# Two graph layers on one core: the second layer's sum over edges as a two by two block product in seven multiplications

## The chip, the core and the metric

The kernel runs on one core of a Trainium2 chip. A core has TensorE (PE; its weight loads are listed apart as PEld), VectorE (DVE), ScalarE (ACT), GpSimd (POOL) and the queue engine SyncE (SP), which here issues nearly all DMAs. The metric is the device time of one execution in microseconds (us), as a median over runs. "Clock" is the share of TensorE's full clock that the chip granted.

## The reference, cut to what matters

There are 1250 nodes with 1024 features and 20000 edges with a weight each.

```python
h = relu(layernorm(x))
x = x + L0(h)      # sigmoid(h @ wenc.T + benc) -> @ conv, weighted sum over edges, + h @ lin.T -> @ wdec.T + bdec
h = relu(layernorm(x))
x = x + L1(h)      # h @ W.T + b, then over edges and self loops: sum of deg^-1/2[row] * deg^-1/2[col] * (row of col)
```

With C the 1250 x 1250 matrix that counts the edges between two nodes (plus the identity, for the self loops), D the diagonal of deg^-1/2 and y = D h, the second layer is D (C y) W.T, plus a term for the bias. The product C y, 1250 x 1250 by 1250 x 1024, is the second layer's sum over edges. It is taken before the product with W.

## The kernel before, in words

All of the work is on tiles of 125 nodes (T = 125, NT = 10 of them). Operands of float32 products are split into a high and a low part (a copy into float32r and a subtraction), and a product takes three passes: high by high, high by low, low by high. Counts are small integers and have no low part, so C y takes two passes.

1. *Encoder, to about 83 us.* Rows are loaded, normed, transposed on TensorE and multiplied by wenc, in five chunks of two tiles. The order of work is written out by hand (`ORDER`).
2. *lin, conv, and the first layer's sum over edges ("agg"), to about 246 us.* Between these products the matrices of weights and of counts are built (`edge_work`: `one_hots` on VectorE, L453 to L461; `adjacency` on TensorE, L479 to L484, then copies on ScalarE and VectorE, L494 to L504). Each 125 columns of counts are stored to HBM (`c_d<-cnt`).
3. *Decoder, to about 308 us.* For each tile t two products with wdec of 512 columns; VectorE adds them to x (L819), takes the statistics (L233), and ScalarE writes relu of the normed row (L249, tile `yf`), copies it as y's high part (L838), and VectorE takes the low part (L799). The sum x is stored to HBM as `x1_d` for the end.
4. *Second layer.* For each of five chunks c of 250 nodes `gathered(c)` multiplies y (stationary, eight blocks of 128 features, ten tiles, two parts) by the chunk's transposed counts `ct` (moving, 250 columns): 160 matmuls on L874. The result z is split (L885, L886), and `finish(c)` multiplies it by w1 (L926, 512 columns), adds and stores (L945). The counts of the next chunk are loaded, transposed on TensorE (L770) and copied (L773) between these products; `bias_factor` (L780) takes a row's sum of counts times the degrees' factor.

Outside of the encoder a planner orders the instructions of each engine by its costs, ahead of the run; on the chip each engine then takes its own list in order. SBUF is given out by two sets of equal slots, 18 big (`big`, 8000 to 8192 bytes a partition) and 14 middle ones (`mid`), in the order of the program: a slot is taken again as soon as its last user has given it back.

```python
def tile(self, shape, dtype, name):
    i = self.free.pop(0)
    t = mem.tile(shape, dtype, tag=f"{self.tag}{i}", name=name)
```

PSUM has eight banks: four for products (`ps_acc`), two for transposes (`ps_t`), two for the edges' matrices (`ps_oh`).

Of the kernel before, what the change touches and what calls it, by code (L numbers as in the profile page):

```python
"""Two pre-norm graph layers on one core.  # L1

Layer 0 (weighted graph convolution inside an encoder and decoder) and layer 1 (a symmetrically
normalised one with self loops) both sum over the same edges, as products with the edges' dense
matrices of weights and of counts.

The matrices are built in SBUF. Destinations go in groups of five, and each group takes a window of
128 consecutive edges, which starts at the first edge that is not below the group when the edges are
sorted by destination. A window's product of one-hot rows, of a source's place among 125 on one side
and of (destination, source's block of 125) times the weight on the other, is the group's columns.  # L10
The weight goes in three bf16 parts that add up to it exactly. The edges that the windows hold are
counted: where they are not all of the edges (unsorted or very uneven destinations), a second path,
for edges in any order, computes the output.

Operands of float32 products are split exactly into a high and a low part of 12 significant bits
each, which TensorE takes in one pass as float32r; counts need no low part.
"""
# [9 lines left out]
F32 = mybir.dt.float32  # L27
# [11 lines left out]
N_BIG = 18  # L39
N_MID = 14  # L40
WARM = 18

# What goes between the encoder's products, after (-1: before) part n of chunk c's: (c, n).
# [30 lines left out]
}  # L74


@with_exitstack
def kernel(
# [36 lines left out]

    const = ctx.enter_context(tc.tile_pool(name="const", bufs=1))
    mem = ctx.enter_context(tc.tile_pool(name="mem", bufs=1))
# [6 lines left out]
    class Slots:  # L124
        """Equal pieces of SBUF, handed out and given back in the order of the program."""

        def __init__(self, tag, n):
            self.tag = tag
            self.free = list(range(n))
            self.of = {}  # L130

        def tile(self, shape, dtype, name):
            i = self.free.pop(0)
            t = mem.tile(shape, dtype, tag=f"{self.tag}{i}", name=name)
            self.of[name] = i
            return t
# [1236 lines left out]
```

## Time and profile before

| | |
|---|---|
| three runs | 523.43, 523.54 and 525.04 us; median 523.54 us |
| profiled execution | 525.9 us from the first to the last instruction; no other time of it is listed |
| PE, PEld busy | 502.7, 456.5 us |
| DVE, ACT, POOL busy | 290.7, 166.1, 73.5 us |
| mean granted TensorE clock | 0.978 |
| C y (L874) | 800 matmuls of 250 columns |
| product with w1 (L926) | 456 matmuls of 512 columns, 48 of 256 |
| DMA | 48.89 MB, mean 93 GB/s |

Matmuls overlap, so the mean duration of one (282 ns for 250 columns) is longer than the time from one to the next; that time is read from the chain of waits, which lists stretches of matmuls with their count and length. The chain follows the work that ended last backwards. A wait names what ended an engine's idle time. In the view by stage each column is the busy time of an engine in that stretch.

### The profile page before, as it was taken

To read this page: it belongs to the slowest core of one execution; us is meant where nothing else is said; L and a number is where in the kernel's file an instruction comes from. 1 tells how busy PE (TensorE), PEld (TensorE's weight loads), DVE (VectorE), ACT (ScalarE), POOL (GpSimd) and SP (SyncE) were. 2 spreads that over 40 slices of the span, in tenths; PEclk is the share of its full clock that TensorE was granted. 3 is DMA by queue.
4 is the path that set the end of the run, shared out by engine and by line. 5 is a ranking of instruction groups with operands and counts; after the bars stand their busy time and mean duration, and the time that the engine had idled before them with its cause. 6 is when DMAs were issued, how large, how long until landed. Compare 5 with 4: busy or idle time off the path is not lost.

```text
span 525.9 us, 9741 instructions
## 1 busy us (share of the span) xinstructions
PE 502.7 (96%) x3954; PEld 456.5 (87%) x3954; DVE 290.7 (55%) x706; ACT 166.1 (32%) x432; POOL 73.5 (14%) x97
## 2 busy tenths in 40 slices
PE   6999997999999996899999998999999999999994
PEld 3999997998889996899777798889889879979984
DVE  6768579657788886662677675544044016115201
ACT  4676453543434343230155543301111111110100
POOL 5723560000000004130012340000000000000000
PEclk9999998999999999699999998999999999999999
DMA  8990120111011122744438452341024015004002
GB/s 294 355 261 22 31 77 0 27 26 26 1 26 26 51 81 64 166 123 106 153 127 255 177 185 67 118 141 68 0 77 131 1 40 167 1 21 115 24 12 73
DMA packets 37781, 48.89 MB, mean 93 GB/s; under 512 B 16608, under 2 KB 26472, under 8 KB 37727
## 3 DMA queue, kind: packets, MB, share of 16 engines
q1 hardware_dynamic: 37407, 47.79, 30.2%
q8 instruction: 33, 0.54, 0.4%
q0 software_dynamic: 320, 0.39, 0.3%
q14 instruction: 21, 0.17, 0.1%
HBM read 34.61 MB, written 17.37 MB: 99 GB/s over the span
## 4 chain that ended last, share of the span: by engine, by line
PE 82%; DVE 7%; DMA 6%; ACT 1%; issue 1%; SPq 0%; POOL 0%; ACTq 0%; DVEq 0%; POOLq 0%
PE pout L926 21%; PE pz L874 16%; PE pagg L318 10%; PE pdec L318 10%; PE penc L318 6%; PE plin L318 5%; PE pconv L318 4%; DMA c_d<-cnt 3%; PE penc L549 2%; PE poh L479 2%; PE pt L258 2%; DVE oh L457 1%; DVE oh L453 1%; PE pct L770 1%; PE poh L483 1%; PE poh L484 1%
## 5 line engine op out<-in xcount | busy, mean ns | idle before, releaser
L926 PE MATMUL pout<-w,z 128*125 128x512 f32 (+1 forms) x504 | 117.6, 388 | 0.0
L926 PEld LDWEIGHTS pout<-w,z 128*125 128x125 f32 x504 | 87.9, 186 | 18.9
L874 PE MATMUL pz<-ct,y 125*128 125x250 f32 x800 | 96.2, 282 | 2.0 <-ACT y L838 2.0
L874 PEld LDWEIGHTS pz<-ct,y 125*128 125x128 f32 x800 | 95.6, 191 | 2.7 <-ACT y L838 2.2
L318 PE MATMUL pagg<-A,h 125*125 125x250 f32 x600 | 76.5, 287 | 0.0
L318 PEld LDWEIGHTS pagg<-A,h 125*125 125x125 f32 x600 | 73.7, 193 | 0.0
L318 PE MATMUL pdec<-wdec,agg 126*125 126x512 f32 x240 | 57.7, 398 | 0.0
L945 DVE SCALAR_TENSOR_TENSOR res<-pout,dinv,res 125x512 f32<-125x512 f32 (+1 forms) x21 | 15.2, 724 | 71.7 <-PE pout L926 71.7
L318 PEld LDWEIGHTS pdec<-wdec,agg 126*125 126x125 f32 x240 | 44.3, 187 | 10.8
L885 ACT CAST z<-pz 128x250 fp32r<-128x250 f32 x40 | 14.3, 370 | 93.0 <-PE pz L874 73.8
L453 DVE TENSOR_TENSOR oh<-cols,eb 128x640 bf16<-128x640 bf16 x50 | 27.0, 539 | 28.1 <-DMA c_d<-cnt 20.6
L479 PE MATMUL poh<-oh 128*128 128x100 bf16 x250 | 28.9, 208 | 10.0 <-DVE A L504 7.3
L494 ACT CAST A<-poh 125x100 fp32r<-125x100 f32 x150 | 25.5, 258 | 40.3 <-PE poh L484 40.1
L318 PE MATMUL penc<-hnh,wenc 128*125 128x250 f32 x256 | 35.4, 288 | 0.0
L886 DVE TENSOR_TENSOR z<-pz,z 128x250 fp32r<-128x250 f32 x40 | 15.9, 413 | 34.7 <-ACT z L885 34.7
L479 PEld LDWEIGHTS <-oh 128*128 128x128 bf16 x250 | 24.1, 97 | 11.6 <-issue 8.0
L773 ACT CAST ct<-pct 125x500 fp32r<-125x500 bf16 (+1 forms) x30 | 15.1, 507 | 55.2 <-PE pct L770 52.4
L318 PEld LDWEIGHTS penc<-hnh,wenc 128*125 128x125 f32 x256 | 32.2, 191 | 0.0
L318 PE MATMUL plin<-hT,lin 125*125 125x250 f32 x240 | 31.0, 285 | 0.0
L318 PEld LDWEIGHTS plin<-hT,lin 125*125 125x125 f32 x240 | 29.4, 191 | 0.0
L318 PE MATMUL pconv<-conv,hT 125*125 125x500 f32 x120 | 28.5, 391 | 0.0
L483 PE MATMUL poh<-oh 128*128 128x50 bf16 x250 | 28.0, 190 | 0.0
(148 smaller groups left out, 689.0 us busy)
## 6 DMA issues: line engine op xcount, KB each, us to landing
x<-in_x_dram SPq DMA_DIRECT2D x14, 512.0 KB
x_d<-x SPq DMA_DIRECT2D x9, 512.0 KB
res<-x_d SPq DMA_DIRECT2D x9, 512.0 KB
out_dram<-res SPq DMA_DIRECT2D x19, 224.0 KB
c_d<-cnt SPq DMA_DIRECT2D x10, 312.5 KB
cr<-c_d SPq DMA_DIRECT2D x10, 312.5 KB
x<-in_x_dram SPq DMA_DIRECT2D x8, 256.0 KB
wencf<-in_wencT_dram SPq DMA_DIRECT2D x4, 500.0 KB
```

What stands on the lines that cost most here:

```text
L258: nc.tensor.transpose(p[:, k, :], xs[t][:T, kk * P : (kk + 1) * P], ident[:T, :T])
L318: nc.tensor.matmul(p, left[i], right[j], start=(part == 0 and n == 0), stop=(part == 2 and n == len(terms) - 1),)
L453: nc.vector.tensor_tensor(pairs(bo), pairs(cols).unsqueeze(1).to_broadcast([P, PB, P // 2, 2]), eb[:, gs].unsqueeze(2).to_broadcast([P, PB ...
L479: nc.tensor.matmul(p[:, g, :], left, mv[:, g, 0:2, :].rearrange("p q m -> p (q m)"), start=True, stop=False,)
L483: nc.tensor.matmul(p[:, g, M:], left, mv[:, g, 2, :], start=False, stop=False)
L494: nc.scalar.copy(hi, whole)
L773: nc.scalar.copy(ct[c][q][:, :, i * T : (i + 1) * T], p[:T, :m, :T])
L874: nc.tensor.matmul(ps[m][:, :CH], y[k][:, s, m * P : (m + 1) * P], ct[c][k // 4][:, k % 4, :], start=(k == 0 and s == 0), stop=(k == NT - ...
L885: nc.scalar.copy(zt[:, 0, m % 2, :], p[:, :CH])
L886: nc.vector.tensor_sub(zt[:, 1, m % 2, :], p[:, :CH], zt[:, 0, m % 2, :])
L926: nc.tensor.matmul(ps[u][:T, : cs.stop - cs.start], z[c][m // 2][:, i, m % 2, (t % 2) * T : (t % 2 + 1) * T], w1[m][:, j, cs], start=(m == ...
L945: nc.vector.scalar_tensor_tensor(x1[t][:, cs], ps[u][:T, : cs.stop - cs.start], dinv[:, t : t + 1], x1[t][:, cs], op0=OP.mult, op1=OP.add,)
```

## The change

C and y are each divided into two by two blocks: C by odd and even tiles of destination and source, y's tiles by odd and even and its features by halves. The product of the blocks is computed by Strassen's scheme in Winograd's form, seven block products in place of eight, with sums of blocks on either side. A block product has five tiles in the sum (NP = 5), 626 columns of counts (625 and one of zeros, W) in pieces of 312 and 314, and is made for four blocks of 128 features (KH = 4).

- *Counts.* The three blocks 11, 21, 22 and the four sums s1 to s4 are made during the decoder, all of them before the products begin: transposes on TensorE, copies on ScalarE, differences s1 and s3 on VectorE, s2 and s4 on GpSimd. `bias_factor` of all tiles moves from the second layer into the decoder.
- *y.* The decoder writes relu straight into one large tile `yz` in float32. The high and low parts are made later, for each of the 28 block products (`prepare`, five products ahead), with the sums of y's blocks on GpSimd first; for the first five the part of tiles 0 to 7 goes ahead of the rest.
- *Products.* `product_step` accumulates the seven products of a feature block in six banks: x and y in `ps_acc`, z in `ps_oh`, with held copies u1 to u3 in SBUF, and writes z in float32, for all 1250 nodes, in the place of y. Only then comes the product with w1, with z split by tile (`split_rows`). w1 is loaded and split during the last seven block products instead of in the decoder and after it.
- *SBUF.* The slots give way to one arena with a list of 322 offsets (`PLAN`), one for each tile in the order of the program, for all stages of the kernel. The code of the encoder, of the edges' matrices and of the first layer is otherwise the same.
- The path for edges in any order, which is in a branch that these inputs don't take, gets some reads and a barrier at its start.

```diff
+class Arena:
+    def tile(self, shape, dtype, name):
+        at = 32 * next(self.places, 0)
...
+        t = self.nc.alloc_sbuf_tensor_at(
+            f"{name}_{len(self.nc.cur_bb.bb.instructions)}", list(shape), dtype, offset=self.base + at
+        )
...
+    NP = NT // 2
+    W = NP * T + 1
...
+    def counts(block, h):
+        q, i = int(block[0]) - 1, int(block[1]) - 1
+        rows_ = cr[2 * h + i]
+        p = ps_t.tile([P, NP, T + 1], BF16, tag="pt", name="pct")
+        for k in range(NP):
+            nc.tensor.transpose(
+                p[:T, k, :T], rows_[:T, (2 * k + q) * T : (2 * k + q + 1) * T], ident_b[:T, :T]
+            )
...
+        if block != "12":
+            nc.scalar.copy(ct[block][:, :, hs], v)
+            return
+        nc.vector.tensor_sub(ct["s1"][:, :, hs], v, ct["11"][:, :, hs])
+        nc.vector.tensor_sub(ct["s3"][:, :, hs], ct["22"][:, :, hs], v)
...
+    def count_sums(s, h):
+        hs = slice(h * T, (h + 1) * T)
+        a, b = {"s2": ("22", "s1"), "s4": ("21", "s2")}[s]
+        nc.gpsimd.tensor_sub(ct[s][:, :, hs], ct[a][:, :, hs], ct[b][:, :, hs])
...
+    for h in range(NP):
+        order += [("11", h), ("21", h), ("22", h)]
+    for h, when in enumerate((9, 13, 16, 18, 19)):
+        order.insert(when, ("12", h))
+    for n, (block, h) in enumerate(order):
+        steps[n].append(lambda block=block, h=h: counts(block, h))
+        if block == "21":
+            steps[n].append(lambda h=h: (bias_factor(2 * h), arena.give(f"cr{2 * h}")))
+        if block == "22":
+            steps[n].append(lambda h=h: bias_factor(2 * h + 1))
...
-            if 5 <= t < 8:
-                counts(0, 2 * (t - 5) + half)
+            for step in steps[2 * t + half]:
+                step()
...
-        yf[t] = mid.tile([T, D], F32, f"yf{t}")
-        y[t] = big.tile([T, 2, D], FR, f"y{t}")
-        relu(yf[t], xt, rs)
-        nc.scalar.copy(y[t][:, 0], yf[t])
+        relu(y[:, :, t], xt.rearrange("p (h m f) -> p m h f", h=2, m=KH), rs)
...
+    count_sums("s2", NP - 1)
+    begin_counts("s4")
+    for h in range(NP):
+        count_sums("s4", h)
+    BLOCKS = {1: ("11", "11"), 2: ("12", "21"), 3: ("s4", "22"), 4: ("22", "s4"), 5: ("s1", "s1"),
+              6: ("s2", "s2"), 7: ("s3", "s3")}
+    Y_SUMS = {"s1": ("21", "22", OP.add), "s2": ("s1", "11", OP.subtract),
+              "s4": ("12", "s2", OP.subtract), "s3": ("11", "21", OP.subtract)}
+    def prepare(m, n, pieces=((0, NP),)):
...
+        for j0, j1 in pieces:
+            for s in {"s2": ("s1", "s2"), "s4": ("s4",), "s3": ("s3",)}.get(name, ()):
+                a, b, op = Y_SUMS[s]
+                nc.gpsimd.tensor_tensor(
+                    sums[m, s][:, j0:j1], y_block(m, a)[:, j0:j1], y_block(m, b)[:, j0:j1], op=op
+                )
+            v, to = y_block(m, name)[:, j0:j1], left[m, n]
+            nc.scalar.copy(to[:, 0, j0:j1], v)
+            nc.vector.tensor_sub(to[:, 1, j0:j1], v, to[:, 0, j0:j1])
...
+    PIECES = ((0, W // 2 - 1), (W // 2 - 1, W))
+    def multiply(m, which, key, first, last):
+        right = ct[BLOCKS[which][1]]
+        for n, (c0, c1) in enumerate(PIECES):
+            p = bank(m, n, key)
+            for j in range(NP):
+                for s in range(2):
+                    nc.tensor.matmul(
+                        p, left[m, which][:, s, j, :], right[:, j, c0:c1],
...
+    def product_step(m, which):
+        if which == 1:
+            multiply(m, 1, "x", True, False)
+            hold(m, "u1", "x")
+        elif which == 2:
+            multiply(m, 2, "x", False, True)
+            put(m, 0, 0, "x")
+        elif which == 6:
+            multiply(m, 6, "y", True, False)
+            hold(m, "u2", "y", "u1")
+        elif which == 5:
+            multiply(m, 5, "z", True, False)
+        elif which == 7:
+            multiply(m, 7, "y", False, False)
+            hold(m, "u3", "y", "u1")
+            put(m, 1, 1, "z", "u3")
...
+        elif which == 3:
+            multiply(m, 3, "z", False, True)
+            put(m, 0, 1, "z", "u2")
...
+        elif which == 4:
+            multiply(m, 4, "y", False, True)
+            put(m, 1, 0, "y", "u1")
...
+    products = [(0, 1), (1, 1), (0, 2)]
+    for m in range(KH):
+        products += [(m, 6), (m, 5), (m, 7)]
+        if 0 < m < KH - 1:
+            products.append((m + 1, 1))
+        products += [(m, 3), (m, 4)]
+        if m + 1 < KH:
+            products.append((m + 1, 2))
+    AHEAD = 5
...
+        if i >= len(products) - 7:
+            for _ in range(2):
+                if len(splits) > len(loads):
+                    k = splits.pop(0)
+                    split_w1(k, nc.gpsimd if k < KH else nc.vector)
+            for _ in range(2 if i < len(products) - 1 else 0):
+                if loads:
+                    load_w1(loads.pop(0))
...
+    def split_rows(t, m0, m1):
+        i, h = t % 2, t // 2
...
+            v, to = z[m][:, :, ns], zs[t][:, :, :, m]
+            nc.scalar.copy(to[:, 0], v)
+            nc.vector.tensor_sub(to[:, 1], v, to[:, 0])
```

## The prediction

> **What bounds the kernel now.** I read the page first, then the chain of waits by line, the waits of TensorE alone, and the busy time by stage.
>
> ```profile
> span 525.9 us, 9741 instructions
> PE 502.7 (96%) x3954; PEld 456.5 (87%) x3954; DVE 290.7 (55%) x706; ACT 166.1 (32%) x432; POOL 73.5 (14%) x97
> ...
> PEclk9999998999999999699999998999999999999999
> ```
>
> TensorE is busy almost throughout, but "busy" counts overlapping matmuls, so the pace is taken from the chain, which walks through one chunk of the second layer:
>
> ```profile
> 344.55 5.62 PE pout L926 x24
> 350.17 18.73 PE pz L874 x160
> ```
>
> 160 matmuls of 250 columns in 18.73 us are 117 ns each; 24 of 512 columns in 5.62 us are 234 ns each. TensorE waits for others in few places (us, times, longest):
>
> ```profile
> PE poh L479 <- DVE A L504: 7.3, 4, 4.7
> PE pt L258 <- ACT x L249: 3.1, 2, 2.2
> PE poh L479 <- DVE oh L461: 2.7, 1, 2.7
> PE pz L874 <- ACT y L838: 2.0, 1, 2.0
> ```
>
> By stage (window; its length; PE, PEld, DVE, ACT, POOL busy; granted clock; DMA):
>
> ```profile
> 77.00:87.00 10.00, 7.33 (x61) 7.12 (x61) 10.00 (x23) 2.17 (x8) 2.95 (x2) 0.83 0.00 0
> 203.00:221.00 18.00, 11.35 (x97) 11.03 (x96) 11.81 (x22) 5.65 (x16) 7.26 (x3) 0.72 0.50 133
> 246.00:314.00 68.00, 68.00 (x351) 56.24 (x350) 48.14 (x92) 28.07 (x30) 17.01 (x14) 1.00 0.52 173
> 314.00:327.00 13.00, 10.99 (x84) 10.78 (x83) 5.06 (x10) 5.31 (x10) 0.12 (x1) 0.87 0.14 34
> 327.00:519.50 192.50, 191.98 (x1216) 169.09 (x1214) 60.41 (x126) 26.18 (x59) 0.00 (x0) 1.00 0.22 69
> ```
>
> So there are three holes, and each brings a spell at half clock. **Hole A** (80 us): 2.7 us idle and 3.4 us at half clock, which costs 1.7: 4.4 us. **Hole B** (205 us): 4.7 + 1.95 idle, and 7 busy us at half clock, 3.5: 10 us. **Hole C** (315 us): 2.0 + 1.7 = 3.7 us. Everything else follows the number of columns. The timelines of VectorE and GpSimd show what hole B is:
>
> ```profile
> 204.94 2.36 POOL L602 TENSOR_TENSOR wdec<-wdec0f,wdec 126x1024 fp32r<-126x1024 f32 x1 [17.15 <-issue]
> ...
> 205.65 2.00 DVE L453 TENSOR_TENSOR oh<-cols,eb 128x640 bf16<-128x640 bf16 x1 [4.27 <-DMA c_d<-cnt]
> 207.57 2.43 DVE L457 TENSOR_TENSOR oh<-cols,ed 128x250 bf16<-128x250 bf16 x1
> ...
> 210.38 2.10 DVE L674 TENSOR_TENSOR agg<-hl,agg 125x250 fp32r<-125x250 f32 x1
> ```
>
> A one-hot first waits 4.27 us for a slot of SBUF that a store of counts still reads; then the same operations that take 0.49, 0.28 and 0.42 us elsewhere take 2.0 to 2.4 us, until a GpSimd split ends. Hole A is the same: the splits of conv and lin hold VectorE between 70 and 80 us.
>
> **What the Trainium skill says.** "SBUF — State Buffer", Who interferes with whom: a VectorE instruction with two SBUF inputs and a GpSimd one that reads SBUF exclude each other, one with an input from PSUM does not. The trace agrees: L674 took 2.10 instead of 0.42 us, L819 (from PSUM) 0.69 us under a split as without. "TensorE: Matmul & The Clock Gate", HAM oscillation: idle gaps over some 3.4 us halve the clock; here 2.0 us did. The same page, LDWEIGHTS: 128 columns load in 128/1.2 = 107 ns, so a 250-column matmul just covers its load and a wider one has room; in the trace the loads of L874 are busy 95.6 of its 96.2 us, those of L926 87.9 of 117.6. "GPSIMD Engine Reference", Instruction dispatch: about 2.5 cycles an element for two inputs; the trace has 2.40 us for 1024, 2.34 ns each, which I use.
>
> **The change part by part.**
>
> *Products.* 800 matmuls of 250 columns go: 800 x 117 = 93.6 us. In come 7 products x 4 feature blocks x 2 pieces x 5 tiles x 2 parts = 560 of 312 or 314 columns. No such width is in the trace. Between 250 (117) and 512 (234), 313 gives 145 ns: 81.2 us. Bounds 142 (2.4 columns per ns plus the 13 ns that 250 shows above it) and 146.5 (in proportion). **-12.4 us** (-14 to -11.6). The 504 matmuls of the last product and the 100 transposes of counts keep their number. The lines added to the path for edges in any order stand in a branch that isn't taken: nothing.
>
> *SBUF.* I laid the offsets of the plan against the order of allocation. The pieces that one-hots take were last held by a count tile at least 11 allocations and releases before, mostly over 20, so the 20.6 us of VectorE waits for count stores (8 times) mostly go. The first half of conv lands where lin's staging was, and its split goes where one-hot 4 was: its split can no longer run ahead of lin's. The split of wdec0 takes one-hot 48's place, so most of the wdec splits come after the one-hots. Hole B: **-9** (0 to -10). Hole A: **-3.5** (0 to -4.4); the conv splits return at about 90 us, two blocks of 2.4 us, under the lead that VectorE then has; without that lead they cost up to 3.
>
> *Decoder.* TensorE: 240 x 0.234 + 100 transposes x 0.055 = 61.7 us. VectorE had 48.1 us in the 68 us window. Off: ten low parts of y, of which nine fall here (11), one split (1.2). On: ten bias factors at 2 x 0.81 + 0.5 (21), ten differences of counts at 625 wide (8), the first pieces of five left operands (5 x 0.69 = 3.5). ScalarE loses ten copies of y (1.05 each) and gains 15 copies of counts (0.68): it stays far from full. VectorE's sum is 68.4 us: it, not TensorE, now ends last, about 3 (start) + 68.4 - 61.7 = 9.7 us after the last decoder product, and the last relu (1.24) follows. Cover: products (0,1), (1,1), which need only even tiles, 5.8 us, and eight matmuls of (0,2), 1.2. Stall about 10.9 - 7 = 4, and half clock 2: **6 us** instead of hole C's 3.7: +2.3. From 0 (planner puts bias factors off, 21 us of them needn't be done here) to 12: s4's five differences (1.6 each) start only when wdec is read out, and each can hold a VectorE operation up to 1.6 us.
> On SP's queue the count loads stand behind the stores of x1, which wait for VectorE's addition. They are issued three halves (9 us) ahead, and count loads took about 4; a backlog over 5 us would make the transposes, in order on TensorE, wait. I put nothing, up to 3.
>
> *Product stage, per feature block 20.3 us of TensorE.* VectorE: 7 low parts of 640 (0.82) + 10 evictions of 313 (0.47) = 10.4; ScalarE 7 x 0.70 + 4 x 0.43 = 6.6; GpSimd four sums x 1.6 = 6.4, which VectorE's low parts exclude: 16.8 of 20.3 at worst. The evictions read PSUM and are not excluded, but stand behind low parts in VectorE's queue. Two pieces in two banks give 1.45 us of slack. In blocks 0 and 3, product 3 follows 7 at once and needs bank z after three additions: 0.2 + 2 x 0.47 + 0.1, about 1.3 us, twice. With 1 for the rest **+3.5** (0 to 12).
>
> *Into the last product.* All eight halves of w1 are now loaded (4.2 MB in 17 us, 247 GB/s; slices above 250 exist) and split in the last six products. VectorE there: 12 evictions 5.6, low parts 1.6, w1 4 x 1.22 = 4.9, rows 2.5, residuals 2.6: 17 us of 17.4, and four GpSimd splits of 2.4 that block it. The two banks of the first units are free and give 2.8 us. **+3** (0 to 7). From there on rows are split at the 40 x (0.37 + 0.41) that L885 and L886 cost now, under 116 us of TensorE.
>
> Sum: -12.4 - 9 - 3.5 + 2.3 + 3.5 + 3 = **-16.1**: a span of 509.8 against 525.9. The profiled execution lies 2.4 above the median of the runs shown (523.54); taken off that, **507.5 us**.
>
> **The rivals.**
> 1. *The holes stay.* The waits for count stores turn into waits for other pieces, or conv's and wdec's splits again meet one-hots. For: VectorE is busy 66 and 100% of the two windows. Against: the waits named have lost their cause. 507.5 + 12.5 = 520.
> 2. *Little new stalls.* Bias factors get put off, the seven products run on. For: VectorE has 60 us in the last 192. Half of the 12.5 us of new stalls: 501; none: 495.
> 3. *Slower: evictions behind GpSimd.* In products 6, 7 and 3 of each block the low part waits for a sum on GpSimd; if it stands ahead of the eviction in VectorE's queue and GpSimd is late, a bank comes free late by 1.6 + 0.94 + 0.3 = 2.8 us, 12 times: +34, 541. It decides from 1.35 us each (16.1 / 12). Against: sums are prepared five products (14.5 us) ahead.
> 4. *The layout doesn't save columns*: if a 313-wide matmul took 167 ns, nothing would be saved: 520. The even slope from 250 to 512 speaks against it.
>
> **How the numbers follow.** The forecast 0.52, rival 1 0.17, rival 2 0.19, rival 3 0.09, rival 4 0.03. From 498 to 520 lie the forecast, most of rivals 1 and 4 and two thirds of rival 2, a little over 0.8. A measurement tells 0.3% (1.6 us) from no change; rival 1 with a larger transition reaches that band. Faster 0.87, same 0.04, slower 0.09.
>
> **What would show it.** 560 matmuls at 145 ns; no wait of one-hots for count stores, and no half clock near 80 and 205 us; VectorE near full in the decoder, and a TensorE gap of some 4 us at its end; gaps of about 1 us where product 3 follows 7 in the first and last block. Wrong if the holes move instead of closing, or if the seven products take over 90 us.

## The result, and the profile after

The changed kernel took 524.27 us (median of 12 runs, 523.03 to 525.85), the one before 523.72 us in the runs beside it (521.62 to 526.27). The ratio is 1.000 (95% interval 0.9982 to 1.0017): no difference that can be measured, where 507.5 us was forecast. The page of the changed kernel begins:

```profile
span 521.5 us, 9414 instructions
...
PE 489.4 (94%) x3714; PEld 440.9 (85%) x3714; DVE 334.0 (64%) x779; ACT 175.2 (34%) x456; POOL 117.8 (23%) x132
...
PEclk9999999999999999999699988999998999999998
```

TensorE has 13 us less to do, VectorE 43 more and GpSimd 44 more. The half clock at 205 us is gone, and a new spell of low clock stands near 250 us; weaker ones follow at 300 to 326 us and near 395 us. (Line numbers moved: a product's matmul is L352 in place of L318, the products of counts and y are L970, the product with w1 is L1108.)

By stage (window; its length; PE, PEld, DVE, ACT, POOL busy; granted clock; DMA share and GB/s):

```profile
77.00:87.00 10.00, 10.00 (x108) 9.84 (x107) 10.00 (x32) 4.77 (x16) 1.79 (x1) 1.00 0.24 70
203.00:221.00 18.00, 16.09 (x209) 15.67 (x209) 11.05 (x38) 10.15 (x36) 7.94 (x4) 1.00 0.37 74
228.00:256.00 28.00, 18.62 (x106) 15.80 (x106) 8.73 (x26) 2.71 (x6) 0.33 (x3) 0.82 0.42 110
256.00:304.00 48.00, 48.00 (x264) 38.64 (x263) 42.50 (x116) 17.50 (x21) 10.19 (x15) 1.00 0.57 195
304.00:318.00 14.00, 8.67 (x42) 7.72 (x42) 13.45 (x15) 5.16 (x10) 14.00 (x11) 0.76 0.18 61
340.00:404.00 64.00, 61.51 (x415) 61.11 (x415) 40.45 (x60) 22.95 (x36) 23.37 (x12) 0.97 0.29 98
```

The first two rows are the places of holes A and B: TensorE is busy 100% and 89% there, against 73% and 63% before. The third row is new: TensorE stands for nine us, and the other engines have little to do (VectorE 8.7 of 28 us, ScalarE and GpSimd 3 together). The fifth is the step from the decoder to the products: GpSimd is busy through all 14 us and VectorE through 13.45. The waits of TensorE alone (us in all, times, longest):

```profile
PE pdec L352 <- DVE hl L706: 9.4, 1, 9.4
PE pz L970 <- DVE cts L816: 4.8, 1, 4.8
PE pz L970 <- ACT zs L1074: 2.5, 1, 2.5
```

After each comes a stretch at lower clock (0.65 from 252 to 257 us, 0.60 from 313 to 318, 0.52 from 395.9 to 399), so each costs more than its idle time. From here on "excess" is TensorE's idle time plus what its matmuls took over their own pace, summed over a stretch. It is 11.4 us around the first of these waits (call it **hole D**), 11.4 us around the second (the **transition**, 300 to 340 us) and 4.1 us at the third (**the hole at w1**); inside the products between 340 and 380 us it is about 0.

Hole D, in the chain of work that ended last:

```profile
230.45 8.89 DMA dinv_d<-dinv
...
239.36 0.28 SPq L849
...
239.68 9.57 DMA dinv_b<-dinv_d
...
250.08 1.54 DVE junk L830 x5
251.62 0.34 DVE hl L706
...
252.00 4.20 PE pdec L352 x10
```

`bias_factor` (L830) needs `dinv_b`, the factors of all nodes on every partition. They are made by a store of 5 KB to HBM and a load that spreads it: 8.89 and 9.57 us, 18.5 together. VectorE's list has factors ahead of L706, the last addition of the first layer, which the decoder's first product needs:

```profile
246.72 0.81 DVE L830 SCALAR_TENSOR_TENSOR junk<-cr,dinv_b 125x625 f32<-125x625 bf16 x1 [15.16 <-DMA dinv_b<-dinv_d]
```

In the kernel before nothing waited for `dinv_b` at this place, as the factors were taken in the second layer. On SP's queue the store had moreover stood behind four loads of counts:

```profile
228.62 1.77 SPq L188 DMA_DIRECT2D cr<-c_d  x4
230.45 0.32 SPq L782 DMA_DIRECT2D dinv_d<-dinv  x1
```

These loads wait for the last store of counts, which ended at 228.56 us; `dinv` itself was ready at 226.8 us, so the order on SP delayed the store by 3.6 us.

The transition, on VectorE and on GpSimd (start, length, line, operation):

```profile
307.31 1.21 DVE L278 SCALAR_TENSOR_TENSOR rs<-mv,rs 125x1 f32<-125x1 f32 x1
...
309.06 1.00 DVE L906 TENSOR_SCALAR rs<-rs,dinv 125x2 f32<-125x2 f32 x1
...
313.40 2.06 DVE L947 TENSOR_TENSOR y<-ys_s,y 125x512 fp32r<-125x512 f32 x1
```

```profile
308.52 6.40 POOL L823 TENSOR_TENSOR cts<-ct,cts 125x625 fp32r<-125x625 f32 x4
```

VectorE operations on one and two elements a partition take 1.2 and 1.0 us, and a low part of 512 takes 2.06 us (0.68 where GpSimd is still): each waits for the end of one of the sums that GpSimd makes back to back (the last of s2, then s4, 1.6 us each, then one of y).

### The profile page after: what moved, and what is told of

Its sections match the earlier page's. It is cut to its first block, busy times and chain, and to the rows that moved or that the text cites. A ratio compares the mean times of both kernels' runs of the same rounds, so it can differ in the third digit from the quotient of the medians.

```text
span 521.5 us, 9414 instructions
## 1 busy us (share of the span) xinstructions
PE 489.4 (94%) x3714; PEld 440.9 (85%) x3714; DVE 334.0 (64%) x779; ACT 175.2 (34%) x456; POOL 117.8 (23%) x132
## 4 chain that ended last, share of the span: by engine, by line
PE 75%; DMA 9%; DVE 7%; issue 2%; ACT 2%; POOL 2%; SPq 1%; ACTq 0%; POOLq 0%; DVEq 0%
PE pout L1108 21%; PE pz L970 11%; PE pagg L352 9%; PE penc L352 9%; PE pdec L352 7%; PE pconv L352 5%; PE plin L352 4%; DVE y L947 3%; DMA c_d<-cnt 3%; PE penc L583 2%; PE poh L513 2%; DMA dinv_b<-dinv_d 2%; DMA dinv_d<-dinv 2%; PE pt L292 1%; DMA wencf<-in_wencT_dram 1%
## 5 line engine op out<-in xcount | busy, mean ns | idle before, releaser
L1108 PE MATMUL pout<-w,zs 128*125 128x512 f32 (+1 forms) x504 | 112.0, 384 | 0.0
L1108 PEld LDWEIGHTS pout<-w,zs 128*125 128x125 f32 x504 | 90.5, 186 | 21.3
L352 PE MATMUL pagg<-A,h 125*125 125x250 f32 x600 | 74.3, 282 | 1.7 <-ACT A L528 1.7
L352 PEld LDWEIGHTS pagg<-A,h 125*125 125x125 f32 x600 | 71.4, 187 | 1.9 <-ACT A L528 1.8
L352 PE MATMUL pdec<-wdec,agg 126*125 126x512 f32 x240 | 62.4, 410 | 9.4 <-DVE hl L706 9.4
L352 PEld LDWEIGHTS pdec<-wdec,agg 126*125 126x125 f32 x240 | 44.5, 192 | 19.3 <-DVE hl L706 9.5
L970 PE MATMUL pz<-cts,y 125*128 125x312 f32 (+1 forms) x320 | 51.2, 314 | 8.4 <-DVE cts L816 4.8
L970 PEld LDWEIGHTS pz<-cts,y 125*128 125x128 f32 x320 | 48.2, 193 | 9.5 <-issue 5.0
L970 PE MATMUL pz<-ct,y 125*128 125x312 f32 (+1 forms) x240 | 39.2, 317 | 1.5 <-DVE y L947 1.3
L970 PEld LDWEIGHTS pz<-ct,y 125*128 125x128 f32 x240 | 36.9, 198 | 2.5 <-DVE y L947 1.8
L352 PE MATMUL penc<-hnh,wenc 128*125 128x250 f32 x256 | 34.4, 284 | 0.0
L352 PEld LDWEIGHTS penc<-hnh,wenc 128*125 128x125 f32 x256 | 31.4, 187 | 0.0
L538 DVE TENSOR_TENSOR A<-poh,A 125x100 fp32r<-125x100 f32 x150 | 26.7, 236 | 5.6 <-ACT cnt L533 5.3
L352 PE MATMUL plin<-hT,lin 125*125 125x250 f32 x240 | 30.2, 282 | 0.0
L352 PEld LDWEIGHTS plin<-hT,lin 125*125 125x125 f32 x240 | 28.7, 187 | 0.0
L352 PE MATMUL pconv<-conv,hT 125*125 125x500 f32 x120 | 28.4, 392 | 0.0
L830 DVE SCALAR_TENSOR_TENSOR junk<-cr,dinv_b 125x625 f32<-125x625 bf16 x20 | 15.7, 806 | 18.8 <-DMA dinv_b<-dinv_d 17.0
```

The lines of the kernel that those rows point to most:

```text
L352: nc.tensor.matmul(p, left[i], right[j], start=(part == 0 and n == 0), stop=(part == 2 and n == len(terms) - 1),)
L538: nc.vector.tensor_sub(lo, whole, hi)
L830: nc.vector.scalar_tensor_tensor(junk, cr[t][:T, q * (N // 2) : (q + 1) * (N // 2)], 1.0, dinv_b[q], op0=OP.mult, op1=OP.mult, accum_out=s ...
L970: nc.tensor.matmul(p, left[m, which][:, s, j, :], right[:, j, c0:c1], start=(first and j == 0 and s == 0), stop=(last and j == NP - 1 and ...
L1108: nc.tensor.matmul(acc[u][:T, : cs.stop - cs.start], zs[t][:, i, half, m, :], w1[k][:, j, cs], start=(m == 0 and half == 0 and n == 0), st ...
```

## The experiments

Each ran beside the kernel before on the same chip; us are medians of four executions (pz_order 20, early_place 6), those of the kernel before of 7 to 23. The groups of runs were on different chips, so two runs are compared by their ratios to the kernel before. The excess is that of one profile, over the 40 us from about the decoder's end (290 to 330 or 300 to 340 us). In the diffs `tc.issue_after(x)` binds the order of what stands inside behind instruction x.

| run | us | before | ratio, 95% interval | excess at the transition |
|---|---|---|---|---|
| layout_only | 516.15 | 523.89 | 0.9855 (0.9798 to 0.9911) | 4.6 |
| late_bias | 514.80 | 523.89 | 0.9807 (0.9754 to 0.9861) | 11.9 |
| no_bias | 516.08 | 523.89 | 0.9827 (0.9777 to 0.9878) | 10.8 |
| pz_order | 522.81 | 523.89 | 0.9989 (0.9968 to 1.0010) | 12.9 |
| swap_pz | 516.51 | 523.80 | 0.9866 (0.9827 to 0.9905) | 14.6 |
| s4_late | 514.36 | 523.80 | 0.9831 (0.9787 to 0.9876) | 12.4 |
| w1_order | 514.59 | 523.80 | 0.9850 (0.9811 to 0.9888) | 11.9 |
| all4 | 512.62 | 523.80 | 0.9796 (0.9755 to 0.9837) | 12 |
| bias_out | 513.86 | 524.46 | 0.9785 (0.9737 to 0.9832) | 10.6 |
| w1_fix | 511.73 | 524.46 | 0.9749 (0.9710 to 0.9787) | 11.5 |
| all6 | 510.30 | 524.46 | 0.9725 (0.9685 to 0.9766) | 11.3 |
| sums_act | 503.64 | 524.53 | 0.9605 (0.9538 to 0.9672) | 4.5 |
| more_first | 512.32 | 524.53 | 0.9772 (0.9701 to 0.9843) | 12.6 |
| late_sums | 517.31 | 526.91 | 0.9799 (0.9759 to 0.9839) | 15.9 |
| sums_dve | 514.50 | 526.91 | 0.9753 (0.9721 to 0.9786) | 13.7 |
| sums_more | 509.72 | 526.91 | 0.9651 (0.9602 to 0.9700) | 9.1 |
| early_place | 509.73 | 525.28 | 0.9702 (0.9658 to 0.9746) | 7.6 |

### One part alone: the layout

The kernel before, with the arena and the offsets of the changed kernel up to the decoder, and offsets of its own for the old second layer.

```diff
-            t = mem.tile(shape, dtype, tag=f"{self.tag}{i}", name=name)
+            t = nc.alloc_sbuf_tensor_at(
+                f"{name}_{len(nc.cur_bb.bb.instructions)}", list(shape), dtype, offset=BASE + at)
-    big = Slots("big", N_BIG)
-    mid = Slots("mid", N_MID)
+    big = mid = Arena()
...
```

> The kernel before with the arena in place of the two sets of slots: up to the decoder the offsets of the changed kernel's plan, after it a layout of our own; the order of work is the old one, eight products. Theory (the layout closes holes A and B, worth the 13 us by which the changed kernel reaches the decoder earlier): the decoder starts 12 to 14 us earlier than before (233 instead of 246 us), holes A and B are gone, and the total is 510 to 513 us, ratio 0.975 to 0.98. Rival (the 13 us come from something else in the changed kernel, or are lost again because the count loads and the rest only wait for other things): decoder start later than 240 us, total over 518 us.

It took 516.15 us, 7.7 less than the kernel before and less of a gain than expected. In the profiles the decoder begins at 233.5 us, as in the changed kernel (233.1), against 246.2 before. Its busy time by stage (columns as above):

```profile
77.00:87.00 10.00, 10.00 (x108) 9.84 (x107) 10.00 (x30) 5.00 (x17) 2.21 (x1) 1.00 0.20 56
203.00:221.00 18.00, 16.30 (x200) 15.89 (x199) 12.27 (x35) 10.25 (x36) 8.72 (x4) 0.91 0.50 132
```

Hole A closes through the layout alone, and hole B for the most part: around them the excess falls from 5.2 to 1.3 us (60 to 110 us) and from 10.6 to 4.0 (195 to 232 us). The waits of VectorE for stores of counts, the named cause of hole B, mostly go (kernel before, changed kernel, layout_only):

```profile
DVE oh L453 <- DMA c_d<-cnt: 20.6, 8, 4.3
DVE oh L487 <- DMA c_d<-cnt: 3.3, 3, 1.7
DVE oh L456 <- DMA c_d<-cnt: 2.1, 2, 1.3
```

The profile pair shows 12.3 us (525.9 to 513.6), the medians 7.7. Most of the difference is in the kernel before: its profiled span of 525.9 stands for about 527.7 us in time (the kernels after have 1.8 us of time outside the span), 4 above its median. Where in that execution the 4 us lie isn't known, as the kernel before was profiled once. They may lie in the holes; or at the start, where the pair differs by another 3.1 us up to 60 us, and where the runs below differ by more than that (1.8 to 7.0 us of excess) without an edit there. What the rest of the change does is then the step from 516.15 to 524.27 us: it *loses* 8.1.

### Hole D: the bias factors

```diff
         if block == "21":
-            steps[n].append(lambda h=h: (bias_factor(2 * h), arena.give(f"cr{2 * h}")))
+            steps[max(n, 4 + 2 * h)].append(lambda h=h: (bias_factor(2 * h), arena.give(f"cr{2 * h}")))
...
-            nc.vector.tensor_add(xt[:, cs], xt[:, cs], p[:T, :])
-            for step in steps[2 * t + half]:
-                step()
+            added = nc.vector.tensor_add(xt[:, cs], xt[:, cs], p[:T, :])
+            with tc.issue_after(added.ins):
+                for step in steps[2 * t + half]: step()
```

> The changed kernel with each bias factor bound on VectorE behind the decoder's addition of its step, and the first four of them put to steps 4 to 7. All bias factors stay in the decoder. Theory (hole D of 9.4 us idle and 2 us at half clock is the wait of the first bias factors for dinv's way through HBM, ahead of the last addition of the first layer in VectorE's queue): the wait before the first decoder product falls under 1 us, the total falls by 8 to 11 us to 513 to 516 us. Rival (the decoder is bound by VectorE's volume, so the work that stood idle only moves to its end): hole D goes, but the transition to the products grows by as much, total within 3 us of 524.

It took 514.80 us, 9.5 less than the changed kernel's median. Hole D is gone: the wait for `hl` no longer appears, and the decoder runs from 234.9 to 298.1 us, 63.2 us in place of 74.6 (233.1 to 307.7). What is left (late_bias, waits of TensorE; the second is the hole at w1, the others are the transition):

```profile
PE pz L970 <- DVE cts L816: 5.2, 1, 5.2
PE pz L970 <- DVE u L983: 3.0, 1, 3.0
...
PE pz L970 <- DVE y L947: 2.1, 1, 2.1
```

The transition stayed as it was, at 11.9 us. Hole D was therefore not its cause. Is it the volume of the factors, 21 us of VectorE, that makes the transition? This kernel leaves them out and sets the bias factor to zero:

```diff
-            nc.vector.scalar_tensor_tensor(
-                junk, cr[t][:T, q * (N // 2) : (q + 1) * (N // 2)], 1.0, dinv_b[q],
-                op0=OP.mult, op1=OP.mult, accum_out=sp[:, q : q + 1],
-            )
...
+        nc.gpsimd.memset(sc[:, t : t + 1], 0.0)
...
```

> The changed kernel without the bias factors: the 20 multiply-and-sum operations and what follows them are left out and the factor is set to zero, so the second layer's bias is left out of the output. Theory (a wait at the decoder's start, and 21 us of VectorE that make it late at the decoder's end): hole D goes (11 us), and the transition, 11.4 us over TensorE's pace now, falls to 4 to 7: total 506 to 510 us. Rival (the transition is set by GpSimd's sums of counts and by TensorE's own order, not by VectorE's volume): the transition stays above 9 us, total 512 to 515, the same as with the bias factors late.

516.08 us, and a transition of 10.8 us: no. The 21 us don't make the transition, and their place ahead of one addition cost over 9. What the 21 us cost elsewhere can't be read from this total: between 256 and 286 us TensorE now waits 1.8 us for a difference of counts (L817) and 1.3 us for a load of counts, which late_bias doesn't have.

### The transition: order and place

TensorE's list had products (0,6) and (0,5), which need the last tile, between those that need only tiles 0 to 8. The first run puts them behind (0,1), (1,1) and most of (0,2), in the changed kernel:

```diff
-        product_step(m, which)
+        with tc.issue_after(pz_last[3]) if (m, which) in ((0, 6), (0, 5)) else ExitStack(): product_step(m, which)
...
```

> The changed kernel with one edge more: the first products with sums of blocks, (0,6) and (0,5), stand on TensorE behind the first four tiles of products (0,1), (1,1) and (0,2). In the changed kernel two matmuls of product (0,5) stand at TensorE's head at 307.7 us, and the second needs the last difference of counts, ready at 312.8, while product (0,1) has its operands. Theory (TensorE's order makes 4.8 us idle and 3.4 of half clock): the gap at 308 us shrinks to under 1.5 us, and the total falls by 4 to 7 us, to 517 to 520. Rival (VectorE and GpSimd are the bound there and TensorE only waits at a later matmul): total 522 to 525.

522.81 us: within the intervals no gain. The wait changed its name:

```profile
PE pz L970 <- ACT y L946: 5.1, 2, 4.8
```

The left operand of (0,1) lies, by the offsets, over tile 8 of x, so its copy waits for that tile's relu. The next run, on top of late_bias, exchanges it with the operand of (1,1) and keeps the new order:

```diff
-    ('y0_1', 0): 5147, ('y1_1', 0): 4627,
+    ('y0_1', 0): 4627, ('y1_1', 0): 5147,
```

> The late bias factors, and the left operands of products (0,1) and (1,1) exchanged in the plan, with the order of TensorE's first products as before this tried alone. In the changed kernel (0,1)'s operand lies over tile 8 of x, so that its copy waits for tile 8's relu (310 us); now it lies over tile 7, and (0,1) stands first on TensorE. Theory (place and order together make the first stall, 5.2 us idle in the run with late bias factors): TensorE's first wait falls under 1.5 us, part of it comes back a few products later since VectorE is still late: total 3 to 6 us under the 514.8 of late bias factors, 509 to 512. Rival (VectorE's lateness at the decoder's end sets it all): total 513 to 516.

516.51 us. The first 16 matmuls then run at once, and (1,1) waits:

```profile
PE pz L970 <- ACT y L946: 7.7, 2, 7.4
```

The third, on late_bias, binds the sums s4 on GpSimd behind the last tile's power, which that tile's relu needs:

```diff
-        root(mv, rs)
+        rooted = root(mv, rs)
...
-    begin_counts("s4")
-    for h in range(NP):
-        count_sums("s4", h)
+    with tc.issue_after(rooted.ins):
+        begin_counts("s4")
+        for h in range(NP): count_sums("s4", h)
```

> The late bias factors, and the five sums of counts s4 (8.8 us on GpSimd) bound behind the last tile's power on GpSimd. Theory (GpSimd's sums keep VectorE's two-input operations waiting at the decoder's end): VectorE's low parts there take 0.68 us again instead of 1.3 to 2.1, the last tile's statistics come 4 to 6 us earlier, and the total falls by 2 to 5 us from 514.8 to 510 to 513. Rival (the lock only moves with the sums, since they have to be made before product 3): total 513.5 to 516.

514.36 us. The low parts take 0.68 us again between 300 and 305 us, but the last tile's statistics (L278 1.53 us, L906 1.47) and low parts from 308 to 315 us are now held instead: excess 12.4 us. Three repairs of order and place each moved the wait and shortened nothing; with the second the excess is even longer. All of them together, with the one at w1 below:

> All four together: late bias factors, exchanged operands with TensorE's order, late sums s4, w1's low parts behind the evictions. If the four stalls are separate: hole D (-10), transition (-5 to -9), hole at w1 (-4) from 524.3: 501 to 506 us, ratio to before 0.957 to 0.966. If VectorE's volume bounds the transition: 509 to 511.

512.62 us, and the transition still about 12.

### The hole at w1

The timeline of VectorE in the changed kernel shows why TensorE stood for 2.5 us:

```profile
393.73 1.65 DVE L636 TENSOR_TENSOR w<-w_6f,w 128x1024 fp32r<-128x1024 f32 x1 [2.92 <-ACT w L635]
395.31 0.86 DVE L983 TENSOR_TENSOR u<-pz,u 128x312 f32<-128x312 f32 x2
```

VectorE waits 2.92 us for ScalarE's copy of the piece w1_6, which waits for its load, and behind it in the list stand the evictions (L983) that free TensorE's bank. (The list of waits names a copy on ScalarE, `zs`, which ended at about the same time; in late_bias the same wait bears the name of L983.) The first run binds the low part of a piece behind the latest eviction before it:

```diff
+                    with tc.issue_after(evicted[0].ins): split_w1(k, nc.gpsimd if k < KH else nc.vector)
...
```

> The late bias factors, and the low parts of w1 bound on VectorE behind the last eviction of the product before. Theory (the hole before the last products, 384 us in that run, is an eviction that stands behind a low part of w1 on VectorE, which waits for ScalarE's copy and so for w1's load): the wait of 3 us goes, the stretch 380 to 400 loses 3.5 to 4.5 us, total 510.5 to 511.5. Rival (the row parts on ScalarE, behind the copies of w1, are what TensorE needs next): the wait moves to the first matmuls with w1, total 513.5 to 515.5.

514.59 us; the edge reached one product too early, so the low part still stood ahead, and a wait of 2.3 us stayed: it tested nothing. The second takes that piece one product later as well:

```diff
-            for _ in range(2):
+            for _ in range((0, 2, 2, 1, 3, 0, 0)[i - len(products) + 7]):
...
```

> The late bias factors, and the split of w1_6 made one product later, behind the evictions of product (3,7); the run tried before this left that low part ahead of them, so that it didn't test the theory. Theory (an eviction waits on VectorE behind w1_6's low part, which waits for ScalarE and the load): the wait of 2.3 to 3.2 us before the last products falls under 1 us, the stretch 380 to 400 loses 3 to 4 us, total 511 to 512. Rival: the wait moves to the first matmuls with w1, total 513.5 to 515.5.

511.73 us, 3.1 less than late_bias (which ran on another chip; by the ratios, 0.9749 against 0.9807, 3.0), and between 380 and 400 us the excess fell from 4.8 to 0.7 us.

### The transition: what bounds it

Two more runs take VectorE's load away. bias_out takes tiles 5 to 9's factors during the product with w1, with their counts loaded again:

```diff
-            steps[max(n, 4 + 2 * h)].append(lambda h=h: (bias_factor(2 * h), arena.give(f"cr{2 * h}")))
+            steps[max(n, 4 + 2 * h)].append(lambda h=h: (bias_factor(2 * h) if h < 3 else None, arena.give(f"cr{2 * h}")))
...
+        if t == 2:
+            for k in range(5, NT): bias_factor(k)
...
```

> The late bias factors, and those of tiles 5 to 9 taken out of the decoder: their counts and dinv are loaded a second time when the last product has been made, and the factors are made in the product with w1, where VectorE is busy a third of the time. Nothing is left out. Theory (VectorE's volume at the decoder's end is one of three causes of the transition, with TensorE's order and GpSimd's sums): VectorE's last addition of the decoder comes 2 us after TensorE instead of 4, and the stretch 290 to 340, 11.9 us over TensorE's pace with the late factors, falls to 8 to 10: total 511 to 513. Rival (only order and place count): total 514 to 516. A third possibility is that the second loads or the factors stall the product with w1: then the stretch after 395 shows a wait.

513.86 us, transition 10.6. all6 is late_bias with the five repairs bias_out, swap_pz (with the order of pz_order), s4_late and w1_fix:

> All of them together: late bias factors with tiles 5 to 9 in the product with w1, exchanged left operands and TensorE's order, s4 behind the last power, w1_6 split one product later. If three causes stand side by side in the transition and each hides the others, now that all are eased together the stretch 290 to 340 falls from 11.9 to 3 to 6 us and with the hole at w1 (3.5) the total is 503 to 507. If something else is the bound there (the last differences of counts, relu of tile 8): 508 to 511.

510.30 us; transition 11.3. Then all6 with the ten sums s2 and s4 left out, where ScalarE copies one of their terms instead:

```diff
-        nc.gpsimd.tensor_sub(ct[s][:, :, hs], ct[a][:, :, hs], ct[b][:, :, hs])
+        nc.scalar.copy(ct[s][:, :, hs], ct[a][:, :, hs])
```

> All of the former changes together, and the ten sums of counts s2 and s4 replaced on ScalarE by copies of their first operand, so that the sums are left out and the products with them are not what they should be: 15.4 us of GpSimd go, 7 us of ScalarE come. Theory (VectorE's operations with two inputs in SBUF and GpSimd's sums share one way in, and the two of them together are what the stretch 290 to 330 takes): the stretch falls from 11.3 us over TensorE's pace to under 5, VectorE's powers' followers take 0.15 to 0.2 us instead of 1.5, total 502 to 505. Rival (the chain from the last decoder product through VectorE and ScalarE to the first operands sets it): over 9 us, total 508 to 511.

503.64 us, 6.7 less (6.3 by the ratios), and the transition has 4.5 us in place of 11.3. VectorE's smallest operation there, in all6 and then in sums_act (count, busy us, mean ns, idle before):

```profile
L278 DVE SCALAR_TENSOR_TENSOR rs<-mv,rs 125x1 f32<-125x1 f32 x3 | 3.7, 1227 | 0.4 <-POOL rs L274 0.4
```

```profile
L278 DVE SCALAR_TENSOR_TENSOR rs<-mv,rs 125x1 f32<-125x1 f32 x3 | 0.5, 157 | 1.3 <-POOL rs L274 1.3
```

This is the first run in which the stall shrank by more than about one us. The sums, some 15 us of GpSimd that hold VectorE, are the larger part of it. The run takes away the holding and has the sums' results ready earlier, both at once; it doesn't tell them apart. (In its decoder a wait of 2.9 us for a load of counts came up, which the total contains.) Would other work for TensorE cover the sums? more_first is all6 with products (2,1) and (3,1), which need no sum, ahead of (0,6). Their results are held in SBUF and added later by VectorE, and the offsets from the last decoder product on are new:

```diff
-    products = [(0, 1), (1, 1), (0, 2)]
+    products = [(0, 1), (1, 1), (0, 2), (2, 1), (3, 1)]
...
```

> All of the former changes together, and another order of products: (2,1) and (3,1), which need no sums of blocks, ahead of (0,6), with their results held in SBUF and added when (1,2), (2,2) and (3,2) are put; offsets from the last decoder product on laid out anew. Nothing is left out. Theory (after the decoder TensorE lacks operands because sums and low parts are made late, and 5.8 us of work without sums covers as much of it): the stretch from the first product to 330 us loses 3 to 6 us, total 504 to 507. Rival (VectorE's six more additions and the earlier low parts cost what the cover gives, or the first stall stands ahead of every product): 509 to 512.

512.32 us: the stall came at 308 to 323 us, 12.6 us long. Each of these products needs its own low part from the same VectorE. Would VectorE do the sums better (about 0.8 us each in place of 1.6), so that nothing is locked? Once in late_bias and once in all6, there behind the last scaling of a row (L906):

```diff
-        nc.gpsimd.tensor_sub(ct[s][:, :, hs], ct[a][:, :, hs], ct[b][:, :, hs])
+        nc.vector.tensor_sub(ct[s][:, :, hs], ct[a][:, :, hs], ct[b][:, :, hs])
```

> The late bias factors, and the ten sums of counts s2 and s4 on VectorE in place of GpSimd, nothing else. They take 0.8 us each there (as the differences of L816 and L817 do) against 1.54 on GpSimd; 7.9 us more for VectorE, 15.4 us less in which a sum keeps VectorE's two-input operations waiting. Theory (shared way in): the stretch 290 to 340 falls from 11.9 us over TensorE's pace to 6 to 9, total 510 to 513. Rival (VectorE is full there, bias factors included, and 7.9 us more make it later): 516 to 520.

> All of the former changes together (the order of products is the changed kernel's), and the ten sums of counts s2 and s4 on VectorE, s4 behind the last tile's scaling. Nothing is left out. Theory: the stretch 290 to 330 falls from 11.3 us over TensorE's pace to 5 to 8 (4.5 with the sums left out), total 504 to 507, ratio 0.962 to 0.967. Rival: 509 to 513.

Ratios 0.9799 and 0.9753, with late_bias at 0.9807 and all6 at 0.9725: no gain, and the stall grew to 15.9 and 13.7 us. late_sums by stage (columns as above):

```profile
298.00:310.00 12.00, 4.10 (x18) 3.29 (x17) 12.00 (x21) 1.51 (x3) 4.11 (x4) 0.64 0.14 43
```

VectorE is full, 12.00 of 12 us, and TensorE stands for 8. In sums_dve nothing holds the small operations any more (L278 takes 0.15 us, L906 0.22), but the sums s4 stand ahead of low parts that TensorE needs, and with GpSimd's sums of y beside them they take 1.4 us each, not 0.8:

```profile
308.61 6.89 DVE L823 TENSOR_TENSOR cts<-ct,cts 125x625 fp32r<-125x625 f32 x5
```

So on either engine the sums are too much work between the decoder's last tile and the first products. That is a reading of these two runs; how much is amount and how much is place they don't separate. Both levers at once, on sums_dve: the sums s4 on VectorE behind the low parts of the first five products, and the order of more_first.

```diff
-    products = [(0, 1), (1, 1), (0, 2)]
+    products = [(0, 1), (1, 1), (0, 2), (2, 1), (3, 1)]
...
+    with tc.issue_after(low.ins): [count_sums("s4", h) for h in range(NP)]
...
```

> As sums_dve, with products (2,1) and (3,1) ahead of (0,6), and s4 behind the low parts of the first five products. With the lock of the sums of counts gone, the 5.8 us of products without sums should cover what is left: stretch 290 to 330 at 2 to 5 us, total 501 to 504. If it only moves the wait as it did before: 505 to 509.

509.72 us, ratio 0.9651, the lowest but for sums_act, which leaves work out; the transition fell to 9.1 us. What is left is again a place: the operand of (1,1) over tile 8.

```profile
PE pz L971 <- ACT y L946: 5.3, 1, 5.3
```

Moved to where agg had been, with the other offsets from the last decoder product on laid out anew around it:

```diff
-    ('y1_1', 0): 5147,
+    ('y1_1', 0): 2456,
...
```

> As sums_more, with offsets from the last decoder product on laid out once more: the left operand of product (1,1) lies no longer over tile 8 of x but over agg of the chunks before, so that its first four tiles can be copied before tile 8's relu. Nothing is left out. Theory (the wait of 5.3 us after the first 16 matmuls is the copy of (1,1)'s operand behind tile 8's relu, in the same place): the wait falls under 1 us, the stretch 290 to 330 from 9.1 us over TensorE's pace to 3 to 5, ratio to before 0.953 to 0.960. Rival (VectorE, full until 308 us, makes the next operand late in its place): 0.962 to 0.967.

509.73 us, ratio 0.9702. The wait fell to 2.4 us and the transition to 7.6, but the new offsets opened a hole at 370 to 390 us of 3.6 us (a wait of 1.9 for `u`, L983). The intervals of both overlap; neither can be called the better one. Both beat the kernel before and the changed one. In both, TensorE also waits for loads of counts in the decoder (1.1 and 1.7 us), which the changed kernel doesn't.

## Why the prediction was wrong, by its steps

| step | forecast | measured | by |
|---|---|---|---|
| products | -12.4 | -12.4 | 560 at 145 ns in the chain |
| holes A and B | -12.5 | -7.7 | layout_only as a whole, medians |
| hole D | 0 | +9.5 | late_bias, medians |
| transition | +2.3 | +7.6 | 11.4 us of excess, less 3.8 before |
| product stage | +3.5 | about 0 | excess of 340 to 380 us (not blocks 0 and 3) |
| into the last product | +3 | +4.1 | excess; w1_fix takes 3.1 back |
| sum | -16.1 | +1.1 | the medians: +0.5 |

The rows mix medians and the excess of single profiles; that they meet the medians within 0.6 us is partly luck.

**Products: right.** The chain has a stretch of 329 matmuls in 47.68 us, 145 ns each, as interpolated between 250 and 512 columns.

**Holes A and B: mechanism right, size from one execution.** They closed for the most part, by the layout alone; in the profiles the excess falls by 3.9 us at A and 6.6 at B, where 3.5 and 9 were forecast. The step "the profiled execution lies 2.4 above the median" set a span against a time (the time was about 4 above), and moved the base only; it did not ask whether the surplus lay in the very holes that were to close. Medians give 7.7 for the layout; where the rest lay stays open.

**The step that failed: "On: ten bias factors at 2 x 0.81 + 0.5 (21)".** I priced the factors as load on VectorE and put the wait for their input at nothing. For the count loads on SP I asked what waits behind them; for `dinv_b` on VectorE I didn't: L706 stood behind it, and behind that the decoder. The trace before had the number: SP issues the same two there, the load 9.28 us after the store that it waits for, and nobody stands behind them (timeline of SP, kernel before):

```profile
238.96 0.32 SPq L748 DMA_DIRECT2D dinv_d<-dinv  x1
248.24 0.67 SPq L845 DMA_DIRECT2D dinv_b<-dinv_d  x2
```

On SP I put "nothing, up to 3" for the count loads, and they came ahead of dinv's store. late_bias shows the whole at 9.5 us by the medians.

**The transition: mechanism right, the term mis-sized.** VectorE was near full and TensorE stood 4.8 us at the first wait, as "some 4 us" said. But the 6 us left out three things. The products that were counted as cover, (0,1) and (1,1), need low parts themselves, so that cover is work for VectorE, and in TensorE's list two matmuls of (0,5) stood ahead of them, so that none of it ran in the first wait. GpSimd is full for 14 us with sums of counts and of y and holds VectorE's low parts; "each can hold a VectorE operation up to 1.6 us" stood only in the upper end of the range. And the low clock came to some 4 us, beside 7.3 of waits, where 2 and 4 were put. The excess was 11.4 us, just under the upper end of 12. sums_act shows 6.8 us of it (11.3 to 4.5) to go with the sums. Of the 4.5 us that remain without them 2.2 us are waits for the parts of y (L946, L947); that share is read from names of waits and not settled by a run. How much of the load can be moved at all stays open below sums_more's 9.1 and early_place's 7.6 us.

**Product stage: too high as far as it can be read.** Between 340 and 380 us the excess is about 0. But 2.6 of the 3.5 us were gaps after product 7 of the first and the last block, which lie outside of that stretch. The first block runs within the transition. In the last one TensorE ran product 4 behind 7, not 3, and its wait for the additions after 7 is the hole at w1; with w1_fix 0.7 us is left there. Rival 3, evictions behind GpSimd in every block, has no trace: the changed kernel's one late eviction is in the last block, and there VectorE waited for w1's low part.

**Into the last product: size right, mechanism in part.** 4.1 against 3. Low parts do stand ahead of evictions in VectorE's list, as was said of the product stage. But the forecast had VectorE full there, 17 of 17.4 us; it was busy 12.2 of the last 17.4 us of the products and stood 2.92 us for a piece of w1, and that wait was not in the sum.

**The rivals.** The nearest was rival 1, waits that turn into others, with the sentence that with a larger transition it reaches no change. It named other pieces of SBUF and splits as the new waits, and neither came; the large new wait came from a reader that was moved ahead. That the total shows no difference is luck: some 20 us won and some 21 lost, a balance that the prediction didn't foresee.

## What to carry to other kernels

When a step moves ahead in the program, follow each of its inputs to where it was last made: a value that goes out to HBM and back has a latency that no engine's busy time shows, and everything behind its first reader in an engine's list inherits it (here 18.5 us, of which TensorE stood for 9.4). Where TensorE's work is taken off by sums on other engines, add up the stage for VectorE and GpSimd together, since here each sum held VectorE's operations on SBUF, and count the preparation of the work that is meant as cover. And when holes of a single profile are to be closed, ask first how often they are there: here the profile lay 4 us above the median.

## What the runs showed of the hardware that was not expected

- A store of 1250 values of 4 bytes to HBM took 8.89 us and the two halves of the load that spreads them over the partitions (305 KB each as landed) 9.57 us from issue to landing. From the store's issue to that of the load it was 8.9 us with four loads of counts issued just ahead on the queue, and 6.7 us in layout_only, where no load was issued in the 8 us before.
- What VectorE waits for GpSimd does not depend on its own size: one element a partition (L278) took 1.23 us beside back to back GpSimd sums (all6) and 0.16 without (sums_act), so that a chain of small operations can pay most of a GpSimd operation, 1.6 us here, at several steps. The Trainium skill's "SBUF — State Buffer", Who interferes with whom, which the prediction used for operations of hundreds of elements, holds down to these.
- Again less than the 3.4 us of the Trainium skill's "TensorE: Matmul & The Clock Gate", HAM oscillation, was enough to lower the clock: after the wait of 2.5 us at w1 it was 0.52 from 395.9 to 399 us, and the next ten matmuls took 2.94 us, about twice their pace.
